# Pairs of gate tiles and products that wait for places, in a planned graph network kernel

## The chip, the cores and the metric

The kernel runs on one core of a Trainium2 chip. The metric is device time in microseconds (us) of one execution. Lower is better.

## The reference

The input is 128 graphs of 64 nodes with 256 features, and one 64 x 64 adjacency matrix. Four layers follow, each with a residual sum and a norm over the features:

```
x = layernorm(x + L0(x))   # three products with adj*adj and weights, relu between
x = layernorm(x + L1(x))   # eigenvectors U of the graph's Laplacian: U (relu(U^T x W1 + b1) W2 + b2)
x = layernorm(x + L2(x))   # two graph products with relu, then LSTMs over windows of nodes
x = layernorm(x + L3(x))   # attention between the nodes of a graph
```

The LSTM part of layer 2 is what the change is about. For p = 1, 2, 3, 4 the 64 nodes are cut into windows of p nodes; an LSTM with its own weights runs over each window from a zero state, and its last hidden state replaces the window's last node, so each p works on what the one before left:

```
g = x_t @ Wih.T + h @ Whh.T + bias
i, f, gg, o = split(g, 4)
c = sigmoid(f) * c + sigmoid(i) * tanh(gg)
h = sigmoid(o) * tanh(c)
```

## The kernel before, in words

The 8192 rows (graph and node) are 64 tiles of 128 partitions; four tiles form a group, 16 groups in all. Layer 0 of all groups comes first, in a part with its own scheduler, together with the eigenvectors, which are computed on the chip. The diff does not touch that part. It ends at about 860 us.

Layers 1 to 3 are then worked in units: six units of two groups and four (`SINGLE`) of one group. `unit` (L1518) notes the operations of `layer1`, `to_lstm` (the graph products and the LSTMs of p = 1, 2 and 3), the LSTM of p = 4 (`four` for two groups together, `lstm` for one), `from_lstm` and `layer3`. Up to three units (`UNITS`) are under way at once.

Nothing is issued in the order in which it is noted. The class `Plan` (L104) is a planner that runs while the program is built. Each noted operation has an engine, an estimated cost and the operations that it follows. `run` (L158) keeps a clock for each engine, picks again and again the operation that can start first by these estimates, and emits it. So each engine gets a fixed order of instructions, made before the chip runs. Tiles are named by a tag, and each tag has a fixed number of places ("slots"): 8 of `ps` (PSUM banks), 7 of `w`, 4 of `v`, 5 of `gates`, 3 of `c`, 4 of `hs`. A tile gets its place when the first operation that names it is emitted, and gives it back when the last one is done. `candidates` (L168) takes an operation to be able to start once the tags of its tiles without a place have one free (`min(s)`, L178).

A step of an LSTM works on the 256 hidden values in two halves h = 0 and 1 of 128. For each half there is one `gates` tile of 128 x 1024. Two forms of a step occur:

- `lstm` (L1378): for each half and each of the gates i, f, g, o a group of products goes to one bank `pp` (L1407): two with `wih` and, after the first step, two with `whh`. ACT then takes tanh of the bank into the gate tile (L1416); DVE forms c (L1420 to L1425), ACT takes tanh of c into the gate tile (L1426), DVE writes the new hidden state `hs` (L1428).
- `halves` (L1439), for pairs of windows in p = 2 and in p = 4 of two groups: seven products of a fast scheme stand for eight. For each half, `two` (L1464) sends the products to a bank; ACT copies the first to a tile `u1` of tag `v` (L1473), and DVE adds up the four parts of the gate tile from `u1` and the banks (L1474 to L1483). Tanh and the state follow as above.

Before the change an operation of PE names only its bank and its inputs. The gate tile gets its place when the first ACT or DVE operation writes it, and the tile of half 1 when half 1 comes to that point.

The tag `v` is also used by layer 1 (`h` and `z`, L1254), layer 2 (L1286) and layer 3 (L1339 and the transposed attention, L1361).

Of the kernel before, what the change touches and what calls it, by code (L numbers as in the profile page):

```python
# [87 lines left out]
class Tile:  # L88


    def __init__(self, tag, shape, real=None):
        self.tag, self.shape, self.real, self.slot = tag, list(shape), real, None
        self.left, self.until, self.past = 0, 0.0, []

    def part(self):
        free = self.shape[1:]
        return Part(self, np.arange(int(np.prod(free))).reshape(free), (0, self.shape[0]), [])
# [6 lines left out]
class Plan:  # L104
# [16 lines left out]
    def tile(self, tag, shape, real=None):  # L121
        return Tile(tag, shape, real).part()

    def note(self, engine, calls, cost, ready=0.0):

        op = Op()
        op.unit = self.unit
        op.engine, op.calls, op.cost, op.group, op.rank = engine, calls, cost, self.group, len(self.ops)
        op.before, op.after, op.tiles, op.ready, op.start = set(), [], [], ready, None
        for name, args, kw in () if callable(calls) else calls:  # L130
            for i, x in enumerate(list(args) + list(kw.values())):
                if not isinstance(x, Part):
                    continue
                t, write = x.tile, i == 0
                mask = np.zeros(int(np.prod(t.shape[1:])), bool)

                mask[... if t.tag == "ps" and not write else x.at.reshape(-1)] = True
                for other, w, rows, m in t.past:
                    if (w or write) and other is not op and other.start is None and rows[0] < x.rows[1] and x.rows[0] < rows[1] and (m & mask).any():
                        op.before.add(other)  # L140
                t.past.append((op, write, x.rows, mask))
                if t not in op.tiles:
                    op.tiles.append(t)
                    t.left += 1
        op.left = len(op.before)
        for other in op.before:
            other.after.append(op)
        self.ops.append(op)
# [9 lines left out]
    def run(self, units, ways):  # L158

        going, todo, held, left = {}, list(enumerate(units)), {}, {}  # L160
        able = {e: [] for e in self.engines}

        def rank(op):
            if op.engine == "PE" and not todo and len(left) <= LASTS:
                return -left[op.group]
            return op.group or 99

        def candidates(guard):  # L168
            oldest = min([u for u in going if u] or [0])
            best = None  # L170
            for e, ops in able.items():
                first = []
                for op in ops:
                    t = max(self.free[e], op.ready)
                    for tile in op.tiles:
                        if tile.real is None and tile.slot is None:
                            s = self.slots[tile.tag]
                            t = max(t, min(s))  # L178

                            if (guard and op.unit != oldest and  # L180
                                    sum(x < 1e9 for x in s) <= self.MOST.get(tile.tag, 1) - held.get((oldest, tile.tag), 0)):
                                t = 1e9
                    if t < 1e9:
                        first.append((t, op))
                if first:
                    t0 = min(t for t, _ in first)
                    t, op = min((x for x in first if x[0] <= t0 + 0.02), key=lambda x: (rank(x[1]), x[1].rank))
                    if best is None or t < best[0]:
                        best = t, op
            return best  # L190

        while todo or going:
            while todo and len(going) < ways + (0 in going):
                self.unit, f = todo.pop(0)
                self.ops, self.group = [], 0
                f()
                going[self.unit] = len(self.ops)
                for op in self.ops:
                    left[op.group] = left.get(op.group, 0) + 1
                    if not op.left:  # L200
                        able[op.engine].append(op)
            t, op = (candidates(True) if todo or len(left) > LASTS else None) or candidates(False)
            e = op.engine
            for tile in op.tiles:
                if tile.real is None:
                    s = self.slots[tile.tag]
                    tile.slot, tile.unit = s.index(min(s)), op.unit
                    tile.real = self.place(tile.tag, tile.slot, tile.shape)
                    s[tile.slot] = 1e9
                    held[op.unit, tile.tag] = held.get((op.unit, tile.tag), 0) + 1  # L210
            self.emit(op)
            able[e].remove(op)
            op.start = t
            self.free[e] = t + op.cost
            end = t + op.cost + self.LAG[e]
            for tile in op.tiles:
                tile.left -= 1
                tile.until = max(tile.until, end)
                if not tile.left and tile.slot is not None:
                    self.slots[tile.tag][tile.slot] = tile.until  # L220
                    held[tile.unit, tile.tag] -= 1
            for other in op.after:
                other.ready = max(other.ready, t + op.cost + self.OWN[e] if other.engine == e else end)
                other.left -= 1
                if not other.left:
                    able[other.engine].append(other)
            going[op.unit] -= 1
            left[op.group] -= 1
            if not left[op.group]:
                del left[op.group]  # L230
            if not going[op.unit]:
                del going[op.unit]
# [504 lines left out]
P = 128  # L737
# [70 lines left out]
def kernel(  # L808
# [26 lines left out]
    V, S, PE = nc.vector, nc.scalar, nc.tensor  # L835
# [108 lines left out]
    def run(out, pairs):  # L944
        for i, (lhsT, rhs) in enumerate(pairs):
            mm(out, lhsT, rhs, i == 0, i == len(pairs) - 1)
# [205 lines left out]
    def place(tag, slot, shape):  # L1152
# [4 lines left out]
        if tag in ("w", "v", "gates", "c", "hs"):  # L1157
# [3 lines left out]
    plan = Plan({"PE": nc.tensor, "DVE": nc.vector, "ACT": nc.scalar, "POOL": nc.gpsimd, "SP": nc.sync}, place,  # L1161
                {"ps": 8, "w": WIDE, "v": 4, "gates": GATES, "c": CELLS, "hs": OUTS, "att": ATT, "mx": 4, "sm": 4, "st": 4, "mv": 4,
                 "rs": 4, "nm": 4})
    V, S, G, Q = (Noted(plan, e) for e in ("DVE", "ACT", "POOL", "SP"))

# [9 lines left out]
    ways = {}  # L1175
# [13 lines left out]
            V.tensor_sub(S3, a11, a21, ready=ready)  # L1189
            ways[p].append([a11, a12, a22, S1, S2, S3, S4])  # L1190

    def products(calls):

        size = lambda x: x.at.size if isinstance(x, Part) else int(np.prod(x.shape[1:]))
        cost = sum(max(0.001673 * size(c[2]) + 0.003, 0.223) for c in calls)
        plan.note("PE", [("matmul", (o, l, r), {"start": a, "stop": z}) for o, l, r, a, z in calls], cost)

    def run(out, pairs, first=True, last=True):
        n = len(pairs)
        products([(out, l, r, first and i == 0, last and i == n - 1) for i, (l, r) in enumerate(pairs)])  # L1200

    def turns(pairs):
        plan.note("PE", [("transpose", (out, in_, ident), {}) for out, in_ in pairs], 0.109 * len(pairs))
# [174 lines left out]
    def lstm(hT, p, first, nw, c=None, new=None):  # L1378
# [3 lines left out]
        n = 8 * nw  # L1382
        wi, wh, bias = wih[p - 1], whh[p - 1], cbi[:, p - 1, :]
        only, hs = c is not None, None
        for t in range(1 if only else p):
            rows = slice(first + t, first + t + (nw - 1) * p + 1, p)
            xt = [hT[:, k, rows, :] for k in range(2)]
            last = t == p - 1
            names = "figo" if t else "igo"
            if p == 2 and t:  # L1390
                x = [[xt[k][:, 16 * w:16 * w + 16] for w in range(2)] for k in range(2)]
# [1 line left out]
                       lambda h, w: hT[:, h, 32 * w + 1:32 * w + 32:2, :])  # L1393
                return
            gate = []
            for h in range(2):
                G = plan.tile("gates", [P, 1024])[:, :len(names) * n].rearrange("p (q n) -> p q n", n=n)
                gate.append({q: G[:, i] for i, q in enumerate(names)})
            if p > 1 and not t and not only:
                c = plan.tile("c", [P, 512])[:, :2 * n].rearrange("p (h n) -> p h n", h=2)  # L1400
# [2 lines left out]
            for h in range(2):  # L1403
                for q in names:
# [4 lines left out]
                    outs = [(wh[:, k, m], hs[:, k, :]) for k in range(2)] if t else []  # L1409
                    if t and h == 0 and q in names[:2]:  # L1410

                        run(pp, ins, last=False)
                        run(pp, outs, first=False)
                    else:
                        run(pp, ins + outs)
                    S.activation(gate[h][q], pp, AF.Tanh, bias=bias[:, j:j + 1], scale=0.5 if q == "g" else 0.25)  # L1416
                    if q == "g":
                        to = gate[h]["g"] if t or p == 1 else c[:, h, :]
# [20 lines left out]
    def halves(p, x, hs, c, new, rows):  # L1439
# [2 lines left out]

        bias = cbi[:, p - 1, :]

        G = [plan.tile("gates", [P, 1024]).rearrange("p (w m q n) -> p w m q n", w=2, m=2, q=2) for _ in range(2)]
        both = work().rearrange("p (s i n) -> p s i n", s=2, i=4)

        def eights(v):
# [11 lines left out]
        for h in range(2):  # L1460
# [3 lines left out]
            def two(*which):  # L1464

                bank = ps4((P, 2, 2, P))
                for at, i in enumerate(which):
                    for q in range(2):
                        run(bank[:, at, q, :], [(ways[p][s][weight[i]][:, q, h, :], moving[i][s]) for s in range(2)])
                return bank[:, 0], bank[:, 1]  # L1470

            p1, p2 = two(0, 1)
# [9 lines left out]
            p4, _ = two(3)  # L1482
# [115 lines left out]
```

## Time and profile before

| what | us |
|---|---|
| three runs | 2457.05, 2458.80, 2458.94; median 2458.8 |
| the profiled execution | 2457.62 |
| its span, from first to last instruction | 2455.8 |
| PE busy in the span | 2431.6 |
| weight loads (PEld) busy | 2158.3 |
| DVE busy | 1618.6 |
| ACT busy | 1073.0 |
| POOL busy | 137.5 |

PE is TensorE's matmuls, PEld its weight loads, which run beside the matmuls; DVE is VectorE, ACT ScalarE, POOL GpSimd and SP the queue that issues most DMAs. An fp32 product of this kernel shows as two matmul rows and two weight loads. Busy times are of the profiled execution; in the planned part all operations carry one line of the code (L156, where the planner emits), so they are told apart by the tiles that they write and read: `ps<-w,wih` is a product into a bank, `gates<-ps,cbi` an activation from a bank into a gate tile.

### The profile page before, as it was taken

How to read it: one execution, taken by the hardware profiler on the slowest of the kernel's cores; microseconds unless marked ns; L12 is line 12 of the kernel's file. 1: busy time of each engine (PE TensorE's matmuls, PEld its weight loads, DVE VectorE, ACT ScalarE, POOL GpSimd, SP SyncE). 2: the span in 40 equal slices, each digit the busy share in tenths (PEclk: the TensorE clock that was granted, in tenths of full speed). 3: DMA queues.
4: the chain of work that ended last, by engine and by line, in shares of the span. 5: the costliest groups of instructions: out<-in, count | busy, mean ns of one | idle time of the engine just before them, and what ended most of it. 6: DMA issues, size and time to landing. Idle time of an engine off the chain costs nothing.

```text
span 2455.8 us, 40814 instructions
## 1 busy us (share of the span) xinstructions
PE 2431.6 (99%) x15500; PEld 2158.3 (88%) x15500; DVE 1618.6 (66%) x5676; ACT 1073.0 (44%) x2610; POOL 137.5 (6%) x315
## 2 busy tenths in 40 slices
PE   9999999999999999999999999999999999999997
PEld 7888888878887899989989998998998998988996
DVE  6888877778888265584684486477558458374336
ACT  2333433333333354445444445444444444545555
POOL 0000000000000010010010000001001001010002
PEclk9999999999999999999999999999999999999999
DMA  7000000000000020010000001001001000000000
GB/s 227 9 1 18 9 10 10 9 10 9 9 1 1 35 87 1 1 36 1 1 18 18 1 1 35 1 1 36 1 1 35 1 1 18 1 10 1 1 1 27
DMA packets 27972, 42.69 MB, mean 17 GB/s; under 512 B 2944, under 2 KB 22144, under 8 KB 27776
## 3 DMA queue, kind: packets, MB, share of 16 engines
q1 hardware_dynamic: 27424, 39.81, 4.7%
q8 instruction: 122, 2.00, 0.3%
q14 instruction: 74, 0.61, 0.1%
q10 hardware_dynamic: 352, 0.28, 0.0%
HBM read 26.45 MB, written 13.63 MB: 16 GB/s over the span
## 4 chain that ended last, share of the span: by engine, by line
PE 94%; DVE 4%; DMA 1%; ACT 0%; issue 0%; POOL 0%; SPq 0%; ACTq 0%; POOLq 0%; DVEq 0%
PE ps L156 62%; PE ps L940 31%; DVE D L52 1%; DVE X L156 1%; PE pc L296 1%; DMA XA<-in_x_dram 1%; DVE st L156 0%; DVE tw L52 0%; POOL rs L156 0%; DVE w L156 0%; DVE h L52 0%; ACT gates L156 0%; DVE gates L156 0%; DVE u L52 0%; DVE v L156 0%
## 5 line engine op out<-in xcount | busy, mean ns | idle before, releaser
L156 PE MATMUL ps<-w,wih 128*128 128x128 f32 (+2 forms) x4144 | 752.7, 315 | 0.9 <-DVE gates L156 0.9
L156 PEld LDWEIGHTS ps<-w,wih 128*128 128x128 f32 x4144 | 646.5, 191 | 37.0 <-issue 6.7
L156 ACT ACTIVATE gates<-ps,cbi 128x168 f32<-128x168 f32 (+2 forms) x832 | 342.2, 417 | 361.2 <-PE ps L156 353.0
L156 PE MATMUL ps<-hs,whh 128*128 128x168 f32 (+1 forms) x1952 | 345.1, 291 | 0.0
L156 PEld LDWEIGHTS ps<-hs,whh 128*128 128x128 f32 x1952 | 288.9, 191 | 1.2 <-issue 1.0
L156 PE MATMUL ps<-w,sums 128*128 128x128 f32 x1776 | 237.7, 275 | 0.0
L940 PE MATMUL ps<-aw,h 128*128 128x256 f32 x1024 | 227.2, 379 | 0.0
L156 DVE SCALAR_TENSOR_TENSOR gates<-gates 128x256 f32<-128x256 f32 (+2 forms) x220 | 83.9, 382 | 215.7 <-ACT gates L156 215.1
L156 PEld LDWEIGHTS ps<-w,sums 128*128 128x128 f32 x1776 | 218.1, 192 | 1.5 <-issue 1.2
L940 PEld LDWEIGHTS ps<-aw,h 128*128 128x128 f32 x1024 | 192.9, 190 | 25.9 <-ACT h L949 0.5
L156 ACT ACTIVATE gates<-gates,cbi 128x256 f32<-128x256 f32 x272 | 116.2, 497 | 194.6 <-DVE gates L156 194.6
L949 ACT ACTIVATE h<-h 128x512 f32<-128x512 f32 x128 | 80.4, 629 | 196.3 <-DVE h L52 196.1
L156 DVE TENSOR_TENSOR gates<-gates,ps 128x256 f32<-128x256 f32 x340 | 128.4, 417 | 19.4 <-PE ps L156 14.4
L940 PE MATMUL ps<-ss,tw 128*128 128x256 f32 x512 | 117.9, 380 | 0.0
L940 PE MATMUL ps<-ss,aw 128*128 128x256 f32 x512 | 117.3, 379 | 0.0
L940 PE MATMUL ps<-m,aw 128*128 128x256 f32 x512 | 117.1, 380 | 0.0
L156 DVE SCALAR_TENSOR_TENSOR c<-gates,c 128x256 f32<-128x256 f32 (+2 forms) x156 | 57.1, 366 | 87.2 <-ACT gates L156 87.0
L940 PE MATMUL ps<-aw,m 128*128 128x512 f32 x256 | 114.6, 593 | 0.0
L156 DVE TENSOR_TENSOR gates<-v,ps 128x256 f32<-128x256 f32 x136 | 55.6, 417 | 80.7 <-ACT v L156 49.9
L940 PEld LDWEIGHTS ps<-ss,aw 128*128 128x128 f32 x512 | 96.6, 190 | 12.8
L940 PEld LDWEIGHTS ps<-ss,tw 128*128 128x128 f32 x512 | 96.3, 190 | 12.9 <-issue 0.2
L940 PEld LDWEIGHTS ps<-m,aw 128*128 128x128 f32 x512 | 95.6, 190 | 12.6 <-issue 0.5
(314 smaller groups left out, 3734.7 us busy)
## 6 DMA issues: line engine op xcount, KB each, us to landing
out_dram<-X SPq DMA_DIRECT2D x64, 128.0 KB, 1.8
rest<-XA SPq DMA_DIRECT2D x10, 512.0 KB, 2.6
X<-rest SPq DMA_DIRECT2D x10, 512.0 KB, 3.3
XA<-in_x_dram SPq DMA_DIRECT2D x18, 256.0 KB, 6.0
wih<-in_c_ih_dram SPq DMA_DIRECT2D x4, 1024.0 KB, 7.4
aw<-in_a_w_dram SPq DMA_DIRECT2D x3, 1024.0 KB, 10.8
X<-in_x_dram SPq DMA_DIRECT2D x12, 256.0 KB, 5.9
whh<-in_c_hh_dram SPq DMA_DIRECT2D x3, 1024.0 KB, 9.4
```

The source lines that it names most:

```text
L52: return getattr(self.engine, name)(out, *args, **kw)
L156: getattr(e, name)(*[real(x) for x in args], **{k: real(v) for k, v in kw.items()})
L296: PE.matmul(out, lhsT, rhs, start=True, stop=True)
L940: PE.matmul(out, lhsT, rhs, start=start, stop=stop)
L949: S.activation(dst, src, AF.Relu)
```

## The change

A tile can be tied to others (`along`). `tiles` makes n tiles of a tag that are tied to each other. When one of them needs a place, the planner asks that as many places as tiles be free (`sorted(s)[len(tile.along)]` in place of `min(s)`), and gives all of them their places at once. Both forms of a step make their two gate tiles this way.

`note`, `products` and `run` take a list `also` of tiles that the operation names without reading or writing them. The operation is then planned only when these tiles have places, and gives them theirs. In `lstm` each group of products names its gate tile; in `halves` each product names its gate tile `a` and the tile `u1`.

The estimates of cost, the numbers of places, the operations and their data stay as they are.

```diff
 class Tile:
         self.left, self.until, self.past = 0, 0.0, []
+        self.along = []
...
+    def tiles(self, n, tag, shape):
+
+        parts = [self.tile(tag, shape) for _ in range(n)]
+        for x in parts:
+            x.tile.along = [y.tile for y in parts if y is not x]
+        return parts
+
-    def note(self, engine, calls, cost, ready=0.0):
+    def note(self, engine, calls, cost, ready=0.0, also=()):
...
+        for x in also:
+            op.tiles.append(x.tile)
+            x.tile.left += 1
...
                         if tile.real is None and tile.slot is None:
                             s = self.slots[tile.tag]
-                            t = max(t, min(s))
+                            t = max(t, sorted(s)[len(tile.along)])
...
-            for tile in op.tiles:
+            for tile in [x for tile in op.tiles for x in [tile] + tile.along]:
                 if tile.real is None:
                     s = self.slots[tile.tag]
                     tile.slot, tile.unit = s.index(min(s)), op.unit
...
-    def products(calls):
+    def products(calls, also=()):
...
-        plan.note("PE", [("matmul", (o, l, r), {"start": a, "stop": z}) for o, l, r, a, z in calls], cost)
+        plan.note("PE", [("matmul", (o, l, r), {"start": a, "stop": z}) for o, l, r, a, z in calls], cost, also=also)
-    def run(out, pairs, first=True, last=True):
+    def run(out, pairs, first=True, last=True, also=()):
         n = len(pairs)
-        products([(out, l, r, first and i == 0, last and i == n - 1) for i, (l, r) in enumerate(pairs)])
+        products([(out, l, r, first and i == 0, last and i == n - 1) for i, (l, r) in enumerate(pairs)], also)
...
             gate = []
-            for h in range(2):
-                G = plan.tile("gates", [P, 1024])[:, :len(names) * n].rearrange("p (q n) -> p q n", n=n)
+            for G in plan.tiles(2, "gates", [P, 1024]):
+                G = G[:, :len(names) * n].rearrange("p (q n) -> p q n", n=n)
                 gate.append({q: G[:, i] for i, q in enumerate(names)})
...
-                        run(pp, ins, last=False)
+                        run(pp, ins, last=False, also=[gate[h][q]])
                         run(pp, outs, first=False)
                     else:
-                        run(pp, ins + outs)
+                        run(pp, ins + outs, also=[gate[h][q]])
...
-        G = [plan.tile("gates", [P, 1024]).rearrange("p (w m q n) -> p w m q n", w=2, m=2, q=2) for _ in range(2)]
+        G = [x.rearrange("p (w m q n) -> p w m q n", w=2, m=2, q=2) for x in plan.tiles(2, "gates", [P, 1024])]
...
-                        run(bank[:, at, q, :], [(ways[p][s][weight[i]][:, q, h, :], moving[i][s]) for s in range(2)])
+                        run(bank[:, at, q, :], [(ways[p][s][weight[i]][:, q, h, :], moving[i][s]) for s in range(2)], also=[a, u1])
```

## The prediction

> **What bounds the kernel now.** I read the page's summary first, then a table of busy time by stage, then PE's waits, then the order of time at PE's longest stop, and the end of the chain last.
>
> ```profile
> span 2455.8 us, 40814 instructions
> PE 2431.6 (99%) x15500; PEld 2158.3 (88%) x15500; DVE 1618.6 (66%) x5676; ACT 1073.0 (44%) x2610; POOL 137.5 (6%) x315
> ...
> PE 94%; DVE 4%; DMA 1%; ACT 0%; issue 0%; POOL 0%; SPq 0%; ACTq 0%; POOLq 0%; DVEq 0%
> ```
>
> TensorE carries 94% of the chain. By stage (columns: stretch, its length, busy time of each engine with instructions, clock, DMA):
>
> ```profile
> 18.20:860.00 841.80, 840.93 (x4019) 691.36 (x4020) 649.97 (x2819) 309.10 (x759) 33.31 (x89) 1.00 0.06 20
> 860.00:2411.00 1551.00, 1548.85 (x11217) 1437.40 (x11217) 932.40 (x2718) 736.25 (x1788) 90.14 (x183) 1.00 0.04 12
> 2411.00:2442.20 31.20, 28.75 (x230) 22.08 (x228) 24.25 (x80) 18.85 (x48) 7.16 (x19) 1.00 0.03 9
> 2442.20:2455.80 13.60, 0.37 (x2) 0.00 (x0) 6.62 (x27) 3.27 (x6) 5.88 (x16) 0.65 0.29 98
> ```
>
> The first stage is layer 0, which the diff doesn't touch. The second is the planned part, where the LSTM lies: 2.15 us of PE idle in 1551. The third is the last units' layer 3, the fourth the last norms without any matmul. What PE waited for in the second stage (us in total, times, longest):
>
> ```profile
> PE ps L156 <- DVE w L156: 1.0, 3, 0.4
> PE ps L156 <- DVE gates L156: 0.9, 1, 0.9
> ```
>
> Busy time hides small stops, since the ends of matmuls are modelled. So I also took the distance between the starts of neighbouring matmuls over the whole second stage and subtracted the usual distance of the shape (0.112 us for a row of 128 columns, 0.142 for 168, 0.216 for 256, 0.43 for 512). Distances more than 0.06 us too long occur 81 times and sum to 10.8 us: 65 of them, 6.1 us, are of the 0.06 to 0.11 kind, mostly where the shape changes; the other 16 make 4.7 us, and four of these 2.5: 1.08 us at 1376, 0.61 at 1261, 0.50 at 2052, 0.34 at 1952. **So at most about 5 us, 0.2% of the time, can be won on PE before the end stage.**
>
> The stop at 1376, in order of time (start, length, engine, line, operation; idle before and what released it in brackets):
>
> ```profile
> 1375.97 0.61 PE L156 MATMUL ps<-ut,v 128*128 128x128 f32 x4
> ...
> 1376.62 0.37 ACT L156 COPY v<-ps 128x256 f32<-128x256 f32 x1 [11.28 <-PE ps L156]
> 1377.02 0.75 DVE L156 TENSOR_TENSOR gates<-v,ps 128x256 f32<-128x256 f32 x2 [10.50 <-ACT v L156]
> 1377.50 0.30 PEld L156 LDWEIGHTS ps<-w,wih 128*128 128x128 f32 x2 [1.11 <-DVE gates L156]
> 1377.50 0.49 PE L156 MATMUL ps<-w,wih 128*128 128x128 f32 x2 [0.92 <-DVE gates L156]
> ```
>
> ACT stood for 11.28 us before the copy at line 1473, DVE for 10.5 us behind it. In the order of the program this copy takes place 2 of the pool "v", which until then holds a layer 1 tile of another group; its last reader is the `ut,v` product that starts at 1375.97. Meanwhile PE filled seven of the eight PSUM banks with this step's products (banks 7, 5, 3, 1, 4, 6, 0; bank 2 is the `ut,v` product) and then had no bank. It is the jam that the second half of the change speaks of. It happens once.
>
> [...] PE reads 99.9% busy in the second stage, weight loads 93%, and only the starts show the 10.8 us. [...] Here the long gap does not repeat (one of 0.9 us in the waits above), so shortage of places is not what holds this kernel. [...] the stop at 1376 shows what a ninth tile costs: 1.08 us.
>
> **The change part by part.** Instructions: PE 7978, DVE 5413, ACT 2486, POOL 317 are the same in both programs, kind by kind; SP's DMAs come in the same order. PE rows with a wait go from 2335 to 2349, DVE's from 4260 to 4248, ACT's and POOL's stay. So the change adds and removes no work: it only moves instructions. Also, a product does not touch a gate tile. Its "wait" is a rule for the planner that writes the order, not a semaphore on the chip; behind a PE instruction nothing new is queued but what the new order puts there. The first 2143 and the last 149 PE instructions are the same in both; so are layer 0 and, on PE, the tail from about 2411.
>
> (a) *Pairs of gate tiles.* I laid the PE products of each order end to end with the distances above, and counted how early each gate place is free before the first result needs it. Before the change it is never late: of 311 the tightest is free 1.3 us early. So taking them in pairs removes no wait: 0 us. The places are held longer (8.1 us on the mean before, 10.4 after), still five places.
>
> (b) *Products wait for the gate tile and for "v".* By the same count three "v" places are late before, by 9.4 us at most, all at 1364 to 1373, and none after. This takes the stop at 1376 away: -1.1 us. What is late next is nothing on PE: in the new order other work stands there, and the next short cover is far off.
>
> (c) *Everything else is dealt anew.* Per product I counted the cover: how much PE work lies between the end of the ACT or DVE work that it needs (durations from the rows, such as 0.37 us for an activation of 128 columns, 0.42 us for a DVE operation of 256, and 0.2 us from PE to ACT) and its own turn, no queue on ACT and DVE assumed (places counted in PE work, up to 10 us ahead of the trace's times). Covers below zero by more than 0.1 us, before 2411: six before, at 1260, 1373 to 1374 (three), 2042 and 2398, and two after, at 2059 (0.47 us: `v` copied by ACT, read at once by layer 1) and 2398 (the same 0.38). The 0.61 and 0.50 us stops of before are in that list and would not come back at those places; the 2059 one is new: +0.5. Covers below 0.5 us: 81 before, 102 after; in the stretch of 2100 to 2411, 20 and 29. There queues decide. The 16 longer stops of before, less the one at 1376, cost 3.6 us at 81 such covers, 0.045 each; 102 would cost 4.6, so +1.0. The 0.6 and 0.5 us stops were layer 3 starts in which PE overtook busy DVE; such starts exist in the new order too, so I book half of the 1.1 us: -0.55, with the bounds -1.1 (both gone) and +1.1 (two more). The stops that hang on queues no row can price ahead; I bound them by -2.5 (all the rest gone) and +4 (twice as many).
>
> (d) *Tail.* The last 149 PE instructions, 98 DVE (names of buffers aside) and 46 ACT instructions are the same. Somewhat earlier DVE's order differs by one residual addition (0.68 us), now behind a norm, and ACT's gates interleave otherwise. The third stage has 31.2 us against 28.75 busy; bounds -1 to +1, taken 0. The fourth is a fixed chain of POOL, ACT and a DMA: 0.
>
> **Sum**, against the profiled run (2457.6 us: span 2455.8 and 1.8 around it): -1.1 + 0.5 + 1.0 - 0.55 + 0 = -0.15, about -0.2. The runs shown are 2457.05 to 2458.94 with median 2458.8; with the profiled one their mean is 2458.1. Less 0.2 this gives 2457.9, so I say 2457.9 us.
>
> **Rivals.** (1) *No measurable change* (my forecast): 2455 to 2462. For it: PE has no idle to give or take but 5 us. (2) *Slower: pairs starve the last units.* From 2164 on only single-group units are left, five gate places give two pairs, so a third step can't start and PE lives on two chains. After the last gate product of a step the chain is: activation 0.4, DVE 0.33 twice, activation 0.33, DVE 0.33, hand-offs of about 0.2, some 2.6 us before the next step's recurrent products. If the other pair doesn't cover it, each of some 25 steps of that stretch loses 0.3 us on the mean: +8 us, 2466; with 0.6 us each, 15 us at most. It decides when cover falls below zero. Against it: the smallest cover of a recurrent product from 2100 to 2411 is 0.19 us in both orders, and a row of six at 2115 to 2121 has 0.30 us where a bank is used as soon as it is read; ACT is busy 47% of the second stage, so a queue of 0.3 us is possible there, a steady one not. (3) *Faster: nearly all longer stops vanish with the jam.* 4.7 us less: 2453.4. For it: the list of negative covers shrinks from six to two. Against: most of the 16 stops have covers of 0.3 us and hang on queues. (4) *It does nothing of what it says*: the jam at 1376 could return elsewhere, since "v" is held longer (12.8 to 15.6 us on the mean): 2459, inside the first case.
>
> **How the numbers follow.** Within 0.2% (4.9 us of 2458.8, which is about what a measurement can tell from no change): case 1 and 4, 0.87. Slower, case 2: 0.09. Faster, case 3: 0.04. The range of 2454.0 to 2463.0 is the sum with most of the bounds of (c) and (d) in one direction (-4 and +5), reaches to the edge of case 3 and leaves out case 2's middle.
>
> **What would show it.** Right: PE idle in the planned stage again near 2 us; no wait of PE or its loads for `gates` near 1376; ACT's wait for `v` no longer has an 11 us member; a stop of about 0.5 us near 2059; the same tail of 45 us after the last LSTM product. Wrong: PE waits for `hs` or `gates` repeated in 2100 to 2411 (case 2), or a tail longer or shorter than 45 us by more than 2.

## The result and the profile after

The changed kernel takes 2461.58 us (median of 19 runs, 2460.0 to 2462.97); the kernel before takes 2458.63 us beside it (19 runs, 2456.92 to 2459.75). The ratio is 1.0014 with a 95% interval of 1.0008 to 1.002: slower by 3 us, small but there. The profiled execution took 2462.19 us (span 2460.4) against 2457.62 (span 2455.8) before; it holds a drop of TensorE's clock (0.61 and 0.54 in two stretches of 2 us) worth some 1.5 us that the one of before has not (last section), so the two differ by more than the medians.

The page's summary of the changed kernel, to be laid beside the one shown of before:

```profile
span 2460.4 us, 40796 instructions
PE 2433.4 (99%) x15500; PEld 2160.6 (88%) x15500; DVE 1619.6 (66%) x5676; ACT 1072.8 (44%) x2610; POOL 137.8 (6%) x315
...
PE 91%; DVE 6%; ACT 1%; DMA 1%; issue 0%; POOL 0%; SPq 0%; ACTq 0%; POOLq 0%; DVEq 0%
```

The engines execute the same work (x15500, x5676, x2610, x315 on both pages), but 3% of the chain has gone from TensorE (PE) to VectorE (DVE) and ScalarE (ACT): PE waited for them. By stage behind layer 0, which is as before (stretch, length, busy time with instructions of PE, PEld, DVE, ACT, POOL, then clock and DMA):

```profile
860.00:2413.50 1553.50, 1547.63 (x11211) 1437.34 (x11210) 932.39 (x2716) 734.96 (x1786) 89.73 (x182) 1.00 0.04 12
2413.50:2446.80 33.30, 30.86 (x235) 24.05 (x233) 25.13 (x82) 19.68 (x49) 7.68 (x20) 0.95 0.03 9
2446.80:2460.40 13.60, 0.35 (x2) 0.00 (x0) 6.60 (x27) 3.27 (x6) 5.91 (x16) 0.67 0.29 98
```

In the planned stage PE is idle for 5.87 us where it was 2.15 before. (The cut at 2413.50 lies some 0.6 us earlier in the work than the one at 2411.00 before, amid products without a stop.) What PE waited for from 860 to 2410 us (us in total, times, longest):

```profile
PE ps L169 <- DVE w L169: 2.0, 4, 1.1
PE ps L169 <- DVE hs L169: 1.3, 1, 1.3
PE ps L169 <- ACT att L169: 1.2, 1, 1.2
PE ps L169 <- ACT w L169: 0.7, 1, 0.7
PE ps L169 <- ACT v L169: 0.3, 1, 0.3
```

The wait for `gates` of before, the jam at 1376, is gone. In its place stand waits for `hs`, `w` and `att`: ordinary inputs that came late.

Below, a *long stop* is what the prediction counted 16 of: two neighbouring matmuls whose starts lie over 0.11 us further apart than their shape needs, after layer 0 (from 845 us on) and before 2409. Before they sum to 4.71 us, after to 9.02 us. Half of the latter is four stops that before has not: 1.43 us at 1099 (`hs`), 1.36 at 1492 (`att`), 0.85 at 1840 (`w`), 1.24 at 2274 (`w`).

The first of them in order of time, DVE's instructions and then PE's (start, length, engine, line, operation; idle before and releaser in brackets):

```profile
1098.71 0.46 DVE L169 SCALAR_TENSOR_TENSOR X<-ps,sm,X 128x256 f32<-128x256 f32 x1
1099.08 0.18 DVE L169 BATCH_NORM_AGGREGATE mv<-st 128x2 f32<-128x6 f32 x1
1099.17 0.46 DVE L169 SCALAR_TENSOR_TENSOR X<-ps,sm,X 128x256 f32<-128x256 f32 x1
1099.54 0.75 DVE L169 BATCH_NORM_STATS2 st<-X 128x6 f32<-128x256 f32 x2
1100.19 0.17 DVE L169 BATCH_NORM_AGGREGATE mv<-st 128x2 f32<-128x6 f32 x1
1100.27 0.40 DVE L169 SCALAR_TENSOR_TENSOR hs<-gates 128x256 f32<-128x256 f32 x1
```

```profile
1095.90 1.99 PE L169 MATMUL ps<-w,v 128*128 128x256 f32 x8
...
1099.07 0.39 PE L169 MATMUL ps<-w,wih 128*128 128x128 f32 x2
1100.73 0.49 PE L169 MATMUL ps<-hs,whh 128*128 128x128 f32 x2 [1.27 <-DVE hs L169]
```

`hs` is the last operation of one group's LSTM step. It has no wait on its own line; it stands behind the layer 3 sums (`X<-ps,sm,X`) and the norm (`st`, `mv`) of another group. A busy table over the 10.7 us up to the stop says that DVE had no gap in which to catch up:

```profile
1090.00:1100.70 10.70, 9.46 (x60) 8.57 (x58) 10.70 (x36) 3.62 (x8) 2.85 (x6) 1.00 0.30 99
```

The third busy column is DVE: 10.70 of 10.70 us, although its share of the whole span is 66%. The last input of `hs`, ACT's `gates<-c`, ends at 1096.98 (from 1096.56, 0.42 us), and `hs` starts at 1100.27: for 3.29 us it stands behind layer 3 and norm work that it doesn't need. The stop at 1492 is the same picture with DVE's `v` behind a norm, then ACT's `att` behind `v` (ACT idle for 2.57 us until `v` is done). At the two others too it is DVE that is late: at 1840 ACT gives PE its `w` right after it got DVE's (a sum at 1840.10, behind gate work and copies), and at 2274 `w` stands behind gate work on DVE. ACT itself stood idle for 0.79 us just ahead of 1840.27.

A full DVE makes no stop by itself. Before the change it runs for 11 us or more without a gap six times in the planned stage (14.00 of 14.00 us from 1674.8, for one), and only one of these stretches holds a stop over 0.25 us (0.50 at 2053).

**Where the profiled execution's 4.57 us come from:** long stops +4.31; the end stage +1.5 (a drop of TensorE's clock, last section); the first matmul starts 0.33 us later; stops of 0.06 to 0.11 us -0.6; what is left, about -1.0, was not traced further.

### The profile page after: what moved, and what is told of

Its sections match the earlier page's. It is cut to its first block, busy times and chain, and to the rows that moved or that the text cites. A ratio compares the mean times of both kernels' runs of the same rounds, so it can differ in the third digit from the quotient of the medians.

```text
span 2460.4 us, 40796 instructions
## 1 busy us (share of the span) xinstructions
PE 2433.4 (99%) x15500; PEld 2160.6 (88%) x15500; DVE 1619.6 (66%) x5676; ACT 1072.8 (44%) x2610; POOL 137.8 (6%) x315
## 4 chain that ended last, share of the span: by engine, by line
PE 91%; DVE 6%; ACT 1%; DMA 1%; issue 0%; POOL 0%; SPq 0%; ACTq 0%; POOLq 0%; DVEq 0%
PE ps L169 59%; PE ps L953 31%; DVE gates L169 1%; DVE X L169 1%; DVE D L52 1%; DVE w L169 1%; ACT gates L169 1%; PE pc L309 1%; DVE st L169 1%; DMA XA<-in_x_dram 1%; DVE tw L52 0%; POOL rs L169 0%; DVE c L169 0%; DVE v L169 0%; DVE h L52 0%
## 5 line engine op out<-in xcount | busy, mean ns | idle before, releaser
L169 PE MATMUL ps<-w,wih 128*128 128x168 f32 (+2 forms) x4144 | 755.0, 314 | 1.1 <-DVE w L169 1.1
L169 POOL TENSOR_SCALAR rs<-mv 128x2 f32<-128x2 f32 x96 | 26.5, 276 | 1464.5 <-DVE mv L169 1463.8
L169 DVE SCALAR_TENSOR_TENSOR hs<-gates 128x168 f32<-128x168 f32 (+2 forms) x168 | 58.9, 351 | 74.8 <-ACT gates L169 74.6
## 6 DMA issues: line engine op xcount, KB each, us to landing
aw<-in_a_w_dram SPq DMA_DIRECT2D x3, 1024.0 KB, 10.7
```

The lines of the kernel that those rows point to most:

```text
L169: getattr(e, name)(*[real(x) for x in args], **{k: real(v) for k, v in kw.items()})
```

## The experiments

Three theories stood on record. **A:** the new order deals the same operations in another way, so that some products of PE find their inputs late, because DVE and ACT are full of other groups' layer 3, norms and gates just then, with the operation that is needed behind them (as `hs` above, 3.29 us after its input); which stops come is a matter of the dealing, not of a mechanism of the change. **B:** pairs of gate tiles leave too few steps ready. **C:** products that wait for places leave PE too little choice.

Two facts needed no run, as the planner is deterministic and its order can be read. Pairs of gate tiles alone, with six places, give the order of before without one instruction moved on PE, DVE or ACT; with five places and without the products' waits the planner finds no order: at some point no operation can start. So the two halves of the change belong together. And in the products of `halves`, where only they wait, the gate tile beside `u1` moves nothing: waiting for `u1` alone gives the identical order. (The expectations of `u_01` and `u_025` below call these products layer 3's; `halves` belongs to the LSTMs of layer 2.)

### Part of the change, alone or left out

Only the wait for `u1` (`e3_u1`), the kernel before with

```diff
-run(bank[:, at, q, :], [...])
+run(bank[:, at, q, :], [...], also=[u1])
```

> One part of the change alone: only the products of the fast scheme (halves) name u1; no pairs, no gate tile named. Theory A (queues: the new order gives PE products whose inputs DVE or ACT deliver late because those engines, in order, are full of other groups' layer 3 and norm; which stops come is a matter of how the order is dealt): the 1.1 us stop at 1376 is gone, the other stops over 0.11 us sum to anything from 3 to 9 us, time 2456 to 2462. Theory B (the pairs leave too few steps ready): no pairs here, so only the stop at 1376 goes, stops 3.6 us, 2457.5. Theory C (products that wait for a place leave PE less choice, whatever the tile): between before and after, 2460.

Measured: 2456.39 us (13 runs) beside 2457.47 for before, ratio 0.9996 (0.9988 to 1.0004); long stops 4.1 us. It takes the jam at 1376 away, another stop of 1.13 us stands at 2048 instead, and the time can't be told from before.

The whole change without pairs (`e2_also`):

```diff
-            x.tile.along = [y.tile for y in parts if y is not x]
+            x.tile.along = []
```

> The change without the pairs: products name gate tiles and u1, but the two gate tiles of a step get their places one by one. Theory A: stops of 3 to 9 us in sum at new places, time 2456 to 2463. Theory B: without pairs back to 2457.5, stops 3.6 us. Theory C: as after, 2461.5, stops 9 us.

Measured: 2458.37 us (13 runs), ratio 1.0002 (0.9994 to 1.0011); long stops 7.1 us, of them 1.35 and 0.89 at 1285 and 1287, where neither before nor after has one, and 1.5 us of matmuls behind these two that came at more than their usual distance (the mean granted clock of this execution is 0.997, that of before's is 0.998). By its time the slowdown needs the pairs in this dealing, which alone would fit B; but B also put the long stops at 3.6 us without pairs, and new ones stand here.

The whole change with six gate places (`e9_six`):

```diff
-GATES = 5
+GATES = 6
```

> The whole change with six places for gate tiles in place of five, so that three pairs fit. Theory A: the shortage of places was none; the order is dealt anew, stops of 3 to 9 us, 2456 to 2463. Theory B: the stops that came with the pairs go, stops at most 4 us, 2458 or less. Theory C: as after, 2461.5.

Measured: 2457.38 us (13 runs), ratio 1.0 (0.9992 to 1.0008); long stops 5.0 us. The stop at 1099 shrinks to 0.55, those at 1492, 1840 and 2274 are gone, and one of 0.93 at 2048 is new. By itself this can't tell A from B: a sixth place gives the pairs room and deals anew as well.

### The norm taken out of the queue

`x_no_norm` has the order of the changed kernel, but the last norm after layer 3 is planned and not issued, so the output is not normalised and the end is shorter.

```diff
+            plan.mute = True
             norm(x2, g in ENDING)
+            plan.mute = False
...
-            self.emit(op)
+            if not op.mute:
+                self.emit(op)
```

> The changed kernel in the same order, but the last norm (after layer 3) is left out: its statistics and scaling on DVE and ACT and its two steps on POOL are not issued, so the output is not normalised. Theory A: the stops of 1.43 us at 1099 and 1.36 us at 1492, whose releasers stand on DVE behind these norms, go; those at 1841 (0.85) and 2274 (1.24), where DVE has gate work only, stay. Theories B and C: all four stay.

Measured: 2447.08 us (one run), 15.1 less than the profiled execution of the changed kernel, of which 9.8 lie behind the last LSTM product (1.5 of these are the clock drop of the last section; here the mean granted clock is 1.000). PE's waits from 860 to 2410 us:

```profile
PE ps L170 <- DVE w L170: 1.1, 1, 1.1
PE ps L170 <- ACT w L170: 0.7, 1, 0.7
PE ps L170 <- ACT v L170: 0.3, 1, 0.3
PE ps L170 <- ACT X L170: 0.2, 1, 0.2
```

The waits for `hs` (1.3) and `att` (1.2) are gone, with pairs, waits and PE's order untouched; those at 1840 and 2274, behind gate operations and copies of other steps, stay. (The `X` line is the first stop of the tail, which before and after have too, at 2411 and 2414; here it falls before 2410.) This is what A said and neither B nor C. Long stops fall from 9.02 to 4.82 us; smaller ones that A had not named, as 0.69 at 2179 and 0.43 at 2092, go as well.

### The same operations dealt anew, without and with the change

The planner takes operations that can start within 0.02 us of the earliest as equals and chooses among them by group. This number alone deals anew:

```diff
-min((x for x in first if x[0] <= t0 + 0.02), ...)
+min((x for x in first if x[0] <= t0 + 0.025), ...)
```

`n_b025` is the kernel before with 0.025, `n_b03` the kernel before with 0.03, `n_a03` the changed kernel with 0.03, `u_01` is `e3_u1` with 0.01. To say ahead what each would do I added to the prediction's count what it had left out: each order walked through with one instruction at a time on DVE and ACT, at the durations of the rows, which is an estimate.

> The kernel before with one number of the planner changed (operations that can start within 0.025 us of the earliest count as equals, instead of 0.02): no part of the change is in it, it only deals the same operations anew. Theory A (in-order queues on VectorE and ScalarE; how many products come late is a matter of the dealing): walking this order through with in-order queues at the durations of the profile's rows, an estimate, late products sum to 14.6 us against 7.1 for the order of before and 10.8 for that of after, with stops of 1.2 to 1.3 us near 1447, 1457, 1644, 1654, 1841, 1850 and 2091; so about 2465 us, slower than the change itself. Theories B (pairs leave too few steps ready) and C (products that wait for places): nothing of either is in it, so the time of before, 2457.5 to 2458.6, with long stops near 4.7 us.

> The kernel before with the same number at 0.03 instead of 0.02; no part of the change. Theory A: late products sum to 10.0 us by the same estimate against 7.1 before, with stops near 1096 (about 2), 1272, 1842, 2085 and 2163; about 2460.5 us, within 1 us of the changed kernel. B and C: the time of before, 2457.5 to 2458.6.

> The whole change, with that number at 0.03 instead of 0.02: the pairs and the waits for places are all there, only dealt anew. Theory A: late products sum to 8.1 us by the same estimate against 10.8 with the change as it is, so about 2459 us, 2 to 3 us faster than the changed kernel and near the kernel before. B and C: all that the change makes wait still waits, so 2461.5 us as with the change.

> Of the change only the wait of layer 3's products in halves for u1, and that number at 0.01: the order among some forty dealings that has the fewest late products by the same estimate, 4.3 us against 7.1 before, all but two of them in the last 15 us. Theory A: about 2455.5 us, faster than both kernels by 2 to 3 us and 6 us. B: as before, 2457.5 to 2458.6 (no pairs). C: at least as slow as before, since products wait for places.

| kernel | part of the change | expected by A | measured, us | ratio to before, 95% | long stops, us |
|---|---|---|---|---|---|
| before | none | | 2457.28 (34 runs) | | 4.71 |
| `n_b025` | none | 2465 | 2464.65 (6 runs) | 1.003 (1.0018 to 1.0041) | 13.73 |
| `n_b03` | none | 2460.5 | 2459.8 (13 runs) | 1.001 (1.0001 to 1.0018) | 8.00 |
| `n_a03` | all | 2459 | 2455.93 (13 runs) | 0.9995 (0.9986 to 1.0003) | 5.24 |
| `u_01` | wait for `u1` | 2455.5 | 2456.19 (13 runs) | 0.9995 (0.9987 to 1.0003) | 4.18 |

As causes of the 3 us, B and C fall here. Without any of the change the same work takes up to 7.4 us longer than before, more than twice what the change cost. With all of the change, pairs and waits included, it takes 2455.56 to 2456.4 us, where none of the changed kernel's runs is below 2459.17 (these are times of different chips; beside the kernel before on its own chip the ratio is 0.9986 to 1.0003 for `n_a03` and 1.0006 to 1.0019 for the changed kernel, `a_again` below). The stops came where A had put them: `n_b025` has 1.63, 1.19, 1.63, 1.19, 1.63, 0.97 and 1.27 us at the seven places named, `n_b03` 1.77, 0.99, 1.06, 1.49 and 1.10 at its five. They stand 2 to 9 us later than named. `n_a03` was 3.1 us faster than A said: its stop at 1099 was gone on the chip, and its end stage 1.1 us shorter; the stop at 1492 stayed, with 1.28 us.

The estimate told the two slow orders ahead. It did not tell the good ones apart: `n_a03` should have been slower than before, and `u_01`, with the fewest late products of all by the estimate, faster by 2 to 3 us; neither can be told from before.

PE's waits in `n_b025`:

```profile
PE ps L156 <- ACT w L156: 4.7, 4, 1.5
PE ps L156 <- DVE w L156: 4.4, 5, 1.1
PE ps L156 <- ACT v L156: 1.2, 2, 0.9
```

One of its four waits for ACT's `w`, on DVE, then ACT, then PE:

```profile
1448.12 0.68 DVE L156 TENSOR_TENSOR w<-ps,wide_c_b 128x512 f32<-128x512 f32 x1
```

```profile
1448.84 0.63 ACT L156 ACTIVATE w<-w 128x512 f32<-128x512 f32 x1 [0.42 <-DVE w L156]
```

```profile
1449.52 0.71 PE L156 MATMUL ps<-adT,w 128*128 128x128 f32 x4 [1.47 <-ACT w L156]
```

DVE's sum of `ps` and `wide_c_b` reads a `cw,w` product. The last of these before it started at 1443.52 and took 1.03 us, but the sum comes only at 1448.12, 3.6 us later, behind copies and gate work on a DVE that is busy for 11.90 us on end (from 1443.9). ACT stood idle and waited for it; PE waited for ACT. So here, too, the full queue is DVE's, though PE's wait names ACT.

### Only the queue of VectorE

If the place in the queue is the cause, moving the late operations up should help with all else as it is. `q_a` is the changed kernel with PE's and ACT's orders untouched and seven DVE instructions 1 to 4 places sooner; `a_again` is the changed kernel on the same chip.

```diff
+SOONER = [(1135, 1133), (1137, 1135), (1140, 1137), (3965, 3963), (3967, 3965), (3969, 3967), ...]
...
-            self.emit(op)
+            self.order.append((op, fresh))
...
+        for x, behind in SOONER:
+            line.insert(line.index(behind) + 1, x)
```

> The whole change, with TensorE's and ScalarE's orders as they are; only on VectorE seven instructions go 1 to 4 places sooner in its queue (the product that writes hs behind the stops near 1099 and 1654, and the products that write w behind those near 1840 and 2273), so that 13 others go 1 or 2 places later. Theory A (in-order queues): the stops of 1.43 near 1099 and 1.24 near 2273 shrink by about 1.1 and 0.7, the two others by about 0.2 each; by the durations of the rows the sum is -2.4, so about 2459.3 us against 2461.6 for the change. B (pairs leave too few steps ready) and C (products that wait for places): pairs, waits and TensorE's order are untouched, so 2461.6 us.

> The changed kernel as it is, to stand on the same chip as q_a: 2461.6 us by all theories.

Measured: `q_a` 2460.58 us (21 runs), `a_again` 2460.68 us (21 runs), both with ratio 1.0013 (1.0007 to 1.002 and 1.0006 to 1.0019): no difference. A's size was missed, and the trace says how. At the stops of 1099 and 2274 the operations came sooner, and PE with them. On DVE and then on PE, at the first:

```profile
1098.94 0.39 DVE L173 SCALAR_TENSOR_TENSOR hs<-gates 128x256 f32<-128x256 f32 x1
```

```profile
1099.38 0.49 PE L173 MATMUL ps<-hs,whh 128*128 128x128 f32 x2 [0.15 <-DVE hs L173]
...
1114.89 0.48 PE L173 MATMUL ps<-cw,w 128*128 128x256 f32 x1 [0.58 <-ACT w L173]
```

The stop at 1099 shrank from 1.43 to 0.32 and that at 2274 from 1.24 to 0.58. But PE reached what follows sooner, and there something else was late: 0.74 us at 1114 (the second line, new), 0.52 at 2277 (new), 0.40 at 1703 (new), and 1.34 instead of 0.85 at 1840. Long stops sum to 9.02 us again. At 1114 it is a copy on ACT behind four activations (1.71 us), which had themselves waited 2.04 us for DVE's gates. So moving one instruction up in DVE's queue only handed the stop on: what is short is DVE's time between PE's products.

What helps is an order of PE that puts products which need nothing new where DVE is full. Two kernels above show that at the very stop of 1099. In `n_a03` and `e9_six` the 56 DVE instructions around `hs` (from 16 us before it to 3 us behind) come in the same order as in the changed kernel. This is `n_a03`, DVE as full as in the table of the result (10.70 us), but PE busy throughout:

```profile
1087.20:1097.90 10.70, 10.70 (x68) 9.61 (x66) 10.70 (x36) 4.19 (x9) 2.83 (x6) 1.00 0.30 98
```

```profile
1093.27 1.99 PE L169 MATMUL ps<-w,v 128*128 128x256 f32 x8
...
1095.99 1.06 PE L169 MATMUL ps<-u,X 128*128 128x128 f32 x8
1096.88 1.06 PE L169 MATMUL ps<-w,sums 128*128 128x128 f32 x8
1097.77 0.39 PE L169 MATMUL ps<-w,wih 128*128 128x128 f32 x2
1098.10 0.49 PE L169 MATMUL ps<-hs,whh 128*128 128x128 f32 x2
```

In all three kernels the `hs,whh` product starts 4.83 us after the eight `w,v` rows, whose results the layer 3 sums take (1100.73 less 1095.90 in the changed kernel, 1098.10 less 1093.27 here). PE's work in between differs and DVE's doesn't, so DVE sets that time. What PE's order sets is how many rows it has to do between the two: 14 in the changed kernel, 22 in `e9_six`, 26 in `n_a03`, and the stop is 1.43, 0.55 and 0.10 us. At 0.112 us a row, these rows and the stop make 3.0 us each time. This is one place; the other stops were not taken apart in this way.

### A version that beats both

Some forty dealings (five versions with eight values of that number each) were counted in the same way. `u_025` is `e3_u1` with 0.025, one of the best; `q_u` is `u_025` with seven instructions moved in the queues of DVE and ACT, PE's order kept.

> Of the change only the wait of layer 3's products in halves for u1, with operations that can start within 0.025 us of the earliest counted as equals. Theory A: late products sum to 5.0 us by the estimate from the rows' durations with in-order queues, against 7.1 for before, and the end stage is 0.9 us shorter: about 2454.5 us. The kernel before with the same 0.025 took 2464.65, so by A a wait for u1 and a dealing together are worth 10 us here without any mechanism of their own. B: as before. C: not faster than before.

> u_025 with TensorE's order as it is, and six instructions on VectorE and one on ScalarE sooner in their queues by 1 to 6 places, chosen so that products near 1668, 2042 and in the end stage have their inputs sooner. Theory A: 1.2 to 1.5 us less than u_025, about 2453.3 us, the fastest of all. B and C: as u_025.

Measured: `u_025` 2453.41 us (20 runs, 2452.94 to 2453.96) beside 2457.28 (72 runs), ratio 0.9982 (0.9976 to 0.9989): faster than both kernels, by 3.9 us and by 7.3 us against `a_again`. `q_u` 2453.0 us (21 runs, 2452.48 to 2455.01), with the same ratio and interval: A had said 1.2 to 1.5 us less than `u_025`, it is 0.4 and inside the spread, as for `q_a`. The kernel before with the same number, 0.025, is the slowest of all, 2464.65. Of the 4.45 us by which its profiled execution (2453.17) is shorter than that of before, 1.74 lie behind the start of the last matmul (11.90 us instead of 13.64) and 1.24 in long stops, counted to the end here, since some fall on both sides of 2409 (7.04 us instead of 8.28); the other 1.5 us are spread over shorter stops and the spacing of the matmuls.

## Why the prediction was wrong

It said no measurable change; the change costs 3 us. By its steps:

**(a) Pairs, 0 us: right as far as shown.** With six places the pairs alone move nothing in the order; with five there is no order that has them alone. With the whole change it isn't pairs as such that cost: `n_a03` has them and runs at 2455.93 us.

**(b) The jam, -1.1 us: right for the stop.** The wait for `gates` at 1376 is gone, and gone with the wait for `u1` alone (`e3_u1`), where a new stop of 1.13 us took most of the gain; so that "what is late next is nothing on PE" did not hold there.

**(c) Everything dealt anew, +0.95 us in sum: this step failed.** Its parts with one answer held: the stop near 2059 is there (0.45 us at 2072, 0.47 said), and the layer 3 starts at 1261 and 2052 lost their 0.61 and 0.50 us. What failed is the term for queues: "no queue on ACT and DVE assumed", and then 0.045 us for each of 102 short covers. The long stops should have gone from 4.7 to 4.55 us; they are 9.02, and four single stops of 0.85 to 1.43 us make 4.88 of it. A mean price per cover can't see them: PE's next products are few *and* DVE is full, as in the 10.7 us without a gap before 1099. (The price also took in the two layer 3 starts, which the sum then books once more; without them it is 0.03 us a cover.) The same rows with one instruction at a time on each engine give 10.8 for after and 7.1 for before, an estimate of 3.7 more, where 4.3 were measured; it was worked out only after the result was known. I had written of stops "that hang on queues no row can price ahead"; rows and the order price the large ones: of five orders dealt anew, four came within 1.1 us of what was said ahead and one, `n_a03`, was 3.1 off. They do not price the small ones: `q_a` should have gained 2.3 us and gained nothing, `q_u` 1.2 to 1.5 and gained 0.4.

**(d) The tail, 0 us: right.** From 2409 on PE's stops over 0.06 us sum to 4.59 us in `q_a`, which has the tail of the changed kernel, and 4.60 in before. The 46.5 us from the start of the last LSTM product on in the profiled execution, against 45.0 before, hold 1.5 us of a clock drop that not every execution has.

**The rivals.** Starved last units (2): not seen; from 2100 to 2409 PE never waits for `hs` or `gates`, and its one stop before an LSTM product is the 1.24 us at 2274, for `w`. Faster (3): no. The jam returning elsewhere (4): no wait for `gates` is left. No measurable change (1): its 0.2% was held to be about what a measurement can tell from no change, but with 19 runs of each kernel the interval is 0.06% to each side, and 3 us show. What happened is a case I had not put up as a rival: slower by new stops at other places, with no mechanism of the change behind it. The range held the time because it took the bound of +4 for that term.

**What stays open:** whether this change is better or worse on the mean over dealings. Without it three dealings gave 2457.3, 2464.65 and 2459.8; with it 2461, 2455.93 and (six places) 2457.38. That is too few to say.

## What to carry to other kernels

When an edit changes only the order of already tuned work, count for each product how early its input is ready *behind all the work that stands ahead of it on its engine*. Judge the engines that feed PE by the 10 us ahead of a stop and not by their share of the whole: DVE is busy 66% of the span and was full for the 10.7 us before 1099. And ask what PE has to do meanwhile: with the same DVE work, 12 rows more on PE took that stop from 1.43 to 0.10 us.

Before you credit or blame a small change of order, deal the same work anew in a way that means nothing: here that alone moves the time by +2.5 and +7.4 us, and a verdict of 0.14% says nothing of the idea behind the change. Where a planner is cheap to run, such a count sorts out the bad orders, and the good ones have to be measured: the order with the fewest late products was not faster than before beyond the interval, another (`u_025`) gained 3.9 us. Of the 4.45 us in its profile 1.7 lie behind the start of the last matmul, which the count of late products does not see.

## What the runs showed that was not expected

In at least three of the profiled executions TensorE's granted clock fell for some 3.4 us within the last 45 us. The changed kernel, 2 us at a time (busy PE, clock, DMA):

```profile
2415.00:2417.00 2.00, 0.89 (x7) 1.00 0.00 0
2417.00:2419.00 2.00, 1.74 (x9) 0.61 0.03 8
2419.00:2421.00 2.00, 2.00 (x7) 0.54 0.00 0
```

(At 0.50, the 0.39 and 0.46 missing from 1.00 in the two later stretches make 3.4 us.) From 2417.48 to 2420.73 the matmuls take twice the distance that they have just after: 0.213 us instead of 0.109 for a row of 128 columns, 0.427 instead of 0.216 for 256. These rows cost 1.6 us; the whole stretch from the last LSTM product on is 1.5 us longer than that of before. `a_again` (0.94, 0.50 and 0.71 from 2415 to 2421) and `u_01` (0.50 and 0.66 from 2413 to 2417) show the same in their profiles; before, `q_a`, `q_u`, `u_025`, `n_a03`, `n_b025` and `n_b03` have 1.00 in every stretch from 2413 to 2423. What sets the drop off was not shown. In the changed kernel PE is busy for only 0.89 of the 2.00 us ahead of it, but `q_a` has the same stretch (0.90) and keeps its clock:

```profile
2415.00:2417.00 2.00, 0.90 (x7) 1.00 0.00 0
2417.00:2419.00 2.00, 1.74 (x13) 1.00 0.04 8
2419.00:2421.00 2.00, 2.00 (x13) 1.00 0.02 4
```

The runs of one kernel fall into two groups some 1.5 us apart (the changed one: 8 of 19 runs at 2460.0 to 2461.0, 11 at 2461.3 to 2463.0). The profiled executions with the drop at the end (after 2462.19, `a_again` 2461.55, `u_01` 2457.65) lie in the upper group of their kernel, those of before (2457.62) and `q_a` (2460.75), without it, in the lower. That fits the drop as what parts the groups; no run shows it directly, as only one execution of each kernel has a profile.
